# An attention and expert block on one core: gate rows computed later and stored by POOL, matmuls of ones ahead of the first data, W2 copies moved to VectorE, a re-spaced drain without activation-table changes

## The chip, the core and the metric

The kernel runs on one core of a Trainium2 chip. Five engines read their own instruction streams in order: PE (TensorE, with its weight loads shown as PEld), DVE (VectorE), ACT (ScalarE), POOL (GpSimd) and SP (SyncE, which here only issues transfers). The metric is device time in microseconds (us) of one launch, less is better. The median of 11 runs before the change is 1141.42 us (1139.15 to 1143.66).

## What is computed

32 sequences of 256 tokens with 128 channels pass an attention half and a mixture-of-experts half, both steered by six rows of a small modulation matrix. Cut to what matters:

```python
mod = (silu(c) @ wmod).reshape(32, 6, 1, 128)
sa, ca, ga, sb, cb, gb = mod[:, 0], ..., mod[:, 5]
ga = (2 * (ga >= 0) - 1) * maximum(abs(ga), 0.25)
gb = (2 * (gb >= 0) - 1) * maximum(abs(gb), 0.25)
h = layernorm(x) * (1 + ca) + sa
x = x + ga * attention(h, wq, wk, wv, wo)      # 8 heads, rms norm and rotation of q and k, causal softmax
h = layernorm(x) * (1 + cb) + sb
# experts: 8, hidden size 512, each token goes to its 2 best
scores = softmax(h @ Wr + br); weights = softmax over the two best scores
x = x + gb * sum_e weights_e * (gelu(h @ W1_e + b1_e) @ W2_e + b2_e)
```

All of it is float32 with 8192 tokens in all.

## The kernel before

The 32 sequences form 16 blocks of 512 tokens (`NBLK`). The order in which every engine gets its work is written by hand: the string `PERIOD` lists some 450 steps, each with a key (sequence of the block, group of four heads, q or k, tile of 128 tokens) and a number `-1`, `-2`, `-3` that says how many blocks it runs behind. One pass through the string is one period; the loop makes 17 of them. What stands early in the string stands early in each engine's queue, and since the queues are in order, a step that waits holds all that its engine was given after it.

The steps that matter below: `PJ` (L461, PE) projects q or k of 128 tokens and four heads; `SQ` (L467, ACT) squares it; `XX` (L475, DVE) multiplies it by cosines and sines into a tile `xx` with two buffers; `ROT` (L492, POOL) adds the halves into `rot`, which frees `xx`; `SC` (L509, POOL) scales q; `TR` (L516, PE) transposes `rot`, `ZT` (L522, ACT) copies it out; `S`, `EX`, `AV` (L536, L564, L573 to L575) are scores, exponential and the product with the values; `RES` (L600, L601, POOL) multiplies by the gate row and adds the residual.

Start. `modulate` makes the two rows that the first norm needs (L251). Right behind it `gates_of` multiplies the other four rows (L257, PE), copies them out (L259, ACT), forms the gates in six POOL instructions (L260 to L269) and stores them as `mod_rows` from ACT's queue (L270). SP loads them back per sequence (`LR`, L415), and its queue goes on in the order: two `rows` loads, then `load_rest` with Wr, br, b1 (L229), lanes, rows, then the next sequences. POOL copies b1 into the tile of the expert weights (L232) behind the first `ROT` of the second head group. `turn_values` and `merge_values` (L276 to L284) multiply wv and wo together once.

Experts. Each token's row is stored into DRAM lists by expert, by a POOL scatter (`LS`, L320, 8 per block). From the lengths of the lists two tables are made that say which tile of 256 list rows belongs to which expert: `first_table` on POOL during the last two full periods (L906 to L976 and the `table` function, L919 to L960), `second_table` on DVE later. 71 tiles follow (`tile_step`): SP loads the rows, PE transposes them, four hidden matmuls with W1 (L1081), gelu on ACT (L1082), the product with W2 (L1109), on DVE the bias and the weight (L1086 to L1097), two scatters into `results` by POOL (L320). The expert's W1 is copied to a working tile by ACT (L1047), its W2 by POOL (L1052, 128x640), one tile ahead. The first 41 tiles (`FULL`) take from the first table.

The last block's routing (logits `LG`, `lg`, `mx`, `sub`, `exp`, `sum`, `rcp`, `sc`, then the two picks `s0` to `p1`, the weights `e0`, `e1`, `w0`, `w1`, the places) is laid between the first tiles by the string `DRAIN`, a group a tile. `exp` (L681) and `e1` (L768) use ACT's exponential, whereas the tiles use gelu. The lists of the block before the last are stored there too (`delayed`).

Of the kernel before, what the change touches and what calls it, by code (L numbers as in the profile page):

```python
# [11 lines left out]
F32 = mybir.dt.float32  # L12
# [3 lines left out]
ALU = mybir.AluOpType  # L16
# [3 lines left out]
P = 128  # L20
# [41 lines left out]
| AV.112 EX.113 RD.112 ST.112 H2.0 | AV.113 RD.113 ST.113  # L62
| HT.0 PAY.0 RES.1 HC.0 | M1.1 | M2.1 MB.1 | M3.1 | H2.1 | HT.1 PAY.1 | HC.1 LS.6-1 | LG LS.7-1
| lg mx sub | exp | sum rcp sc s0 | d0 k0 m0 p0 sc2 | s1 d1 k1 m1 e0 | p1 sel e1 | PC w0 w1 pay2
| len place pp | to LS.0 | | LS.1 | | LS.2 | | LS.3 | | LS.4 | | LS.5 | LS.6 | | LS.7
"""
# [3 lines left out]
def kernel(  # L70
# [49 lines left out]
    FW = FC * P  # L120
    LOADS = 4


# [6 lines left out]
    assert DONE[0] <= FULL and (EARLY - LAST[0]) * K * TB > E * (TS - 1)  # L130
    DONE[0] = FULL + E - 1

    const = ctx.enter_context(tc.tile_pool(name="const", bufs=1))
# [28 lines left out]
    minus_half = const.tile([P, 1], F32)  # L162
    nc.vector.memset(minus_half, -0.5)


# [88 lines left out]

    def gates_of(mps):
        pg = mps.tile([B, 4, M], F32, tag="pj", name="pg")
        nc.tensor.matmul(pg, sg, wmod_sb[:, 2 * M :], start=True, stop=True)  # L257
        g = g_sb[0:B, 0:4, :]
        nc.scalar.copy(g, pg)  # L259
        nc.gpsimd.tensor_scalar_add(g[:, 2, :], g[:, 2, :], 1.0)  # L260


        gates = g[:, ::3, :]
        mag, sgn = gate_sb[0:B, 0:2, :], gate_sb[0:B, 2:4, :]
        nc.gpsimd.tensor_scalar(sgn, gates, 0.0, 2.0, ALU.is_ge, ALU.mult)
        nc.gpsimd.tensor_scalar_add(sgn, sgn, -1.0)
        nc.gpsimd.tensor_mul(mag, sgn, gates)
        nc.gpsimd.tensor_scalar_max(mag, mag, 0.25)
        nc.gpsimd.tensor_mul(gates, sgn, mag)  # L269
        nc.scalar.dma_start(mod_rows, g)  # L270

# [62 lines left out]
    with ExitStack() as pa:  # L334
# [68 lines left out]
        class Steps:  # L403
# [276 lines left out]
            def exp(blk):  # L680
                nc.scalar.activation(held["sc", blk], held["sc", blk], AF.Exp)  # L681

# [83 lines left out]
            def e1(blk):  # L766
                e = keep(sm, [P, 2, NTB], "e", blk)
                nc.scalar.activation(e[:, 0], held.pop(("e0", blk)).squeeze(2), AF.Exp)  # L768
                nc.scalar.activation(e[:, 1], e[:, 0], AF.Identity, bias=ones[:, 0:1])

            def w0(blk):
                nc.vector.reciprocal(held["pay", blk][:, :, 0, M + 1], held["e", blk][:, 1])

            def w1(blk):
                pay = held["pay", blk]
                nc.gpsimd.tensor_mul(
                    pay[:, :, 1, M + 1], held.pop(("e", blk))[:, 0], pay[:, :, 0, M + 1]
                )
# [86 lines left out]
        load_table()  # L865
        Steps.LX(0, 0)
        nc.sync.dma_start(cT_sb, cT)
        nc.sync.dma_start(wmod_sb, wmod)
# [6 lines left out]
        for step in first[3:]:  # L875
            step(0, 0)
        gates_of(ps_pj)

# [20 lines left out]
        def small(name, shape, dtype=F32):  # L899
            return tab.tile(shape, dtype, name=name)  # L900

        def tile_counts(eng, counts, blk, full):


            half, whole = 0.5 - 0.5 / TS, 1.5 * 2.0**23
            eng.tensor_scalar(  # L906
                counts, lengths[:, blk, :], 1.0 / TS, -half if full else half, ALU.mult, ALU.add
            )
            eng.tensor_scalar_add(counts, counts, whole)
            eng.tensor_scalar_add(counts, counts, -whole)  # L910

        def table(eng, name, bounds, n):
# [7 lines left out]

            pad = 1 << (S * E - 1).bit_length() - 1
            sums = [small(f"{name}_sums{i}", [P, pad + S * E]) for i in range(2)]
            for i in range(2):
                eng.memset(sums[i][:, 0 : pad + 1], 0.0)
            eng.tensor_copy(sums[0][:, pad + 1 :], counts.rearrange(flat)[:, 0 : S * E - 1])
            yield
            d = 1
            while d < S * E:
                old, new = sums
                eng.tensor_add(new[:, pad:], old[:, pad:], old[:, pad - d : pad - d + S * E])  # L930
                sums = [new, old]
                d *= 2
                if d in (4, 16):
                    yield
            ahead = held[name + "_ahead"] = sums[0][:, pad:].rearrange("p (s e) -> p s e", e=E)
            held[name + "_counts"] = counts
            yield
            nth = tab.tile(shape, F32, tag="nth", name="nth")
            eng.tensor_scalar(nth, ahead, -1.0, lane, ALU.mult, ALU.add)
            is_its = tab.tile(shape, F32, tag="is_its", name="is_its")  # L940
            eng.tensor_sub(is_its, nth, counts)
            eng.tensor_scalar(is_its, is_its, 0.0, None, ALU.is_lt)
            begun = tab.tile(shape, F32, tag="begun", name="begun")
            eng.tensor_scalar(begun, nth, 0.0, None, ALU.is_ge)
            eng.tensor_mul(is_its, is_its, begun)
            yield
# [8 lines left out]
            yield  # L955
            eng.tensor_mul(each, each, is_its.rearrange(flat).unsqueeze(1).to_broadcast([P, 3, S * E]))
            its = small(name + "_its", [P, 3])
# [4 lines left out]
            yield  # L962

        def first_table():
            eng = nc.gpsimd
            bounds = small("full", [P, 3, E])
            eng.memset(bounds[:, 0], 0.0)
            tile_counts(eng, bounds[:, 2], EARLY, True)
            yield
            tile_counts(eng, bounds[:, 1], LAST[0], False)  # L970
            yield

            less = small("less", [P, E])
            eng.tensor_sub(less, bounds[:, 1], bounds[:, 2])
            eng.tensor_scalar_max(less, less, 0.0)
            eng.tensor_sub(bounds[:, 1], bounds[:, 1], less)  # L976
            yield
            yield from table(eng, "first", bounds, lengths[:, EARLY, :])

        def second_table():  # L980
# [10 lines left out]
            for i, blk in enumerate(LAST):  # L991
                tile_counts(eng, bounds[:, i + 1], blk, False)
                if i == 0:
                    eng.tensor_tensor(bounds[:, 1], bounds[:, 1], bounds[:, 0], ALU.max)
                if i % 2 == 0:
                    yield
# [51 lines left out]

        def weights_2(i):
            e = number(i, 1, mybir.EngineType.Pool, E - 1)  # L1050
            w2s[i] = wk2.tile([P, FW + M], F32, tag="sq", name="w2")
            nc.gpsimd.tensor_copy(w2s[i], W2_sb[:, ds(e, 1), :].squeeze(1))  # L1052

# [64 lines left out]
        def tile_step(i, between=()):  # L1118
            if 0 <= i + LOADS < NTI:
                load(i + LOADS)  # L1120
            if 0 <= i + 1 < NTI:
                weights_2(i + 1)
            if 0 <= i < NTI:
                hidden(i, between)
            if 0 <= i + 1 < NTI:
                rows_in(i + 1)
            if 0 <= i + 2 < NTI and i >= 0:
                weights_1(i + 2)
            if 1 <= i:
                rows_out(i - 1)  # L1130
            if 0 <= i < NTI:
                second(i)
# [39 lines left out]
        def issue(steps):  # L1172
# [9 lines left out]
            (0, 0, 1, 1): [(turn_values, 1), (merge_values, 0)],  # L1182
            (0, 1, 0, 0): [(merge_values, 1)],
        }
        waiting, delayed = [], []
        for n in range(NBLK + 1):
            if n == 1:
                load_rest()
            if n == 3:
                load_experts()  # L1190
            for j, (step, key, behind) in enumerate(period):
                blk = n - behind
                if not 0 <= blk < NBLK or (blk == 0 and step in first and key == [0]):
                    pass
                elif blk == 0 and step in (Steps.V, Steps.VC) and waiting is not None:
                    waiting.append((step, key))
                elif n == NBLK and blk == NBLK - 2 and step is Steps.LS:
                    delayed.append((step, key, NBLK - 1 - blk))
                else:
                    step(blk, *key)  # L1200
                if blk == 0 and step is Steps.PJ:
                    for aside, g in besides.pop(tuple(key), ()):
                        aside(ps_s, g)
                    if not besides and waiting is not None:
                        for aside, k in waiting:
                            aside(0, *k)
                        waiting = None
                if NBLK - 2 <= n < NBLK and j % 48 == 47:
# [12 lines left out]
        for i in range(NTI + 1):  # L1221
# [4 lines left out]
            if held.get("lengths"):  # L1226
                next(tables, None)
                next(ends, None)
            issue(delayed[i : i + 1])
            if i + 3 < len(drain):  # L1230
# [83 lines left out]
```

## Time and profile before

| | |
|---|---|
| median of 11 runs | 1141.42 us |
| profiled execution, time | 1140.71 us |
| its span, first to last instruction | 1138.5 us |
| mean granted TensorE clock | 0.994 |
| PE busy | 1098.8 us (97%) |
| POOL busy | 963.5 us (85%) |
| DVE busy | 959.4 us (84%) |
| ACT busy | 870.9 us (76%) |

The page divides the span into 40 equal slices and gives each engine's busy share of a slice as a digit. A row of a timeline reads: start in us, duration in us, engine, line, operation, what is written and from what, the count of merged instructions, and in brackets the idle time before it with what ended it. A row of a table by stages gives, for a stretch of the span, each engine's busy us and the count of its instructions, then the granted clock, the share of the DMA engines and GB/s. A row of a list of waits gives who waited for whom, the total in us, the number of times and the longest.

### The profile page before, as it was taken

Reading aid. Unit: us, or ns where it says so; the run is one execution under the profiler, and the core shown is the slowest. Engines: PE = TensorE matmul, PEld = TensorE weight load, DVE = VectorE, ACT = ScalarE, POOL = GpSimd, SP = SyncE. Lnnn points to the kernel's source line nnn. Section 1 sums busy time; section 2 is a strip of 40 time slices with the busy share of each in tenths; the row PEclk is TensorE's granted clock in tenths of the full one; section 3 lists DMA queues with packets and bytes.
Section 4 is the critical chain, followed back from the end, with each engine's and each line's share of the span. In section 5 each row is a group of like instructions: output and inputs, shape, how many; then the busy total and the mean of one; then the engine's idle time right before and its main releaser. Section 6 shows DMA issues by size and latency. Waiting matters only on the chain.

```text
span 1138.5 us, 22160 instructions
## 1 busy us (share of the span) xinstructions
PE 1098.8 (97%) x6566; PEld 859.4 (75%) x6566; DVE 959.4 (84%) x2582; ACT 870.9 (76%) x2244; POOL 963.5 (85%) x1257
## 2 busy tenths in 40 slices
PE   6999999999999999999999999998998999999994
PEld 3777777777777777777777777676787889999994
DVE  3989999999999999999999999998973465445895
ACT  4878888888878888888878888787875776766762
POOL 5768989898989989898989989998957788877775
PEclk9999999999999999999999999999999999999998
DMA  4005101010000101000000100001002243224785
GB/s 149 1 13 177 33 23 28 18 30 22 24 25 20 31 23 29 17 29 22 24 26 19 31 22 26 17 31 37 13 6 65 66 106 92 79 73 113 230 230 147
DMA packets 70102, 61.69 MB, mean 54 GB/s; under 512 B 8627, under 2 KB 60468, under 8 KB 69984
## 3 DMA queue, kind: packets, MB, share of 16 engines
q1 hardware_dynamic: 52832, 39.09, 12.8%
q0 software_dynamic: 8640, 16.93, 4.4%
q10 hardware_dynamic: 8512, 4.26, 1.3%
q8 instruction: 53, 0.87, 0.3%
q14 instruction: 65, 0.53, 0.2%
HBM read 38.01 MB, written 23.15 MB: 54 GB/s over the span
## 4 chain that ended last, share of the span: by engine, by line
PE 79%; DVE 6%; POOL 6%; DMA 5%; issue 3%; ACT 1%; SPq 0%; POOLq 0%; DVEq 0%; ACTq 0%
PE pj L461 17%; PE s L536 13%; PE ptr L516 9%; PE pj L449 9%; PE py L1109 7%; PE ph L1081 7%; PE o L573 5%; PE o L575 5%; PE o L574 5%; DMA results<-yo,to 2%; DMA y<-results 2%; POOL rot L492 1%; POOL results L320 1%; PE pm L659 1%; POOL rot L509 1%
## 5 line engine op out<-in xcount | busy, mean ns | idle before, releaser
L492 POOL TENSOR_TENSOR rot<-xx 128x512 f32<-128x512 f32 x256 | 323.6, 1274 | 23.5 <-DVE xx L475 14.5
L475 DVE TENSOR_TENSOR xx<-pj,rope_sb 128x1024 f32<-128x1024 f32 x256 | 310.9, 1215 | 12.4 <-ACT sq L467 8.1
L461 PE MATMUL pj<-wqk_sb,hT 128*128 128x512 f32 x512 | 261.0, 597 | 4.1 <-DVE xx L475 4.1
L564 ACT ACTIVATE p<-s,rn 128x256 f32<-128x256 f32 (+1 forms) x512 | 188.1, 422 | 49.2 <-DVE s L557 43.2
L536 PEld LDWEIGHTS s<-zT,zT 128*128 128x128 f32 x1024 | 179.7, 191 | 51.4 <-issue 34.1
L536 PE MATMUL s<-zT,zT 128*128 128x256 f32 (+1 forms) x1024 | 207.6, 328 | 0.0
L467 ACT ACTIVATE sq<-pj 128x512 f32<-128x512 f32 x256 | 153.6, 600 | 55.7 <-PE pj L461 42.7
L320 POOL DMA_INDIRECT results<-yo,to x142 | 145.0, 1021 | 44.2 <-issue 18.0
L1082 ACT ACTIVATE hid<-ph,w 128x256 f32<-128x256 f32 x284 | 124.7, 473 | 75.2 <-PE ph L1081 74.0
L485 DVE TENSOR_REDUCE ss<-sq 128x4 f32<-128x512 f32 x256 | 172.2, 674 | 3.2 <-ACT sq L467 3.2
L516 PEld LDWEIGHTS ptr<-ident,rot 128*128 128x128 f32 x1024 | 120.5, 141 | 54.3 <-issue 34.7
L522 ACT COPY zT<-ptr 128x512 f32<-128x512 f32 x256 | 146.5, 589 | 11.9 <-PE ptr L516 11.9
L320 POOL DMA_INDIRECT lists<-pay,to x128 | 128.6, 1004 | 30.1 <-issue 14.2
L573 PEld LDWEIGHTS o<-vx,p 128*128 128x128 f32 x512 | 87.0, 190 | 87.3 <-issue 39.9
L516 PE MATMUL ptr<-ident,rot 128*128 128x128 f32 x1024 | 146.9, 273 | 1.8 <-POOL rot L492 1.8
L1109 PE MATMUL py<-w,hid 128*128 128x128 f32 x1136 | 138.9, 275 | 3.5 <-POOL w L1052 1.6
L592 DVE SCALAR_TENSOR_TENSOR attn<-o,rd,attn 128x128 f32<-128x128 f32 x448 | 135.7, 344 | 5.3
L1109 PEld LDWEIGHTS py<-w,hid 128*128 128x128 f32 x1136 | 132.5, 192 | 4.5 <-POOL w L1052 3.4
L1081 PE MATMUL ph<-hT,w 128*128 128x256 f32 x568 | 134.7, 380 | 0.0
L449 PE MATMUL pj<-wvo_sb,hT 128*128 128x512 f32 x256 | 132.2, 599 | 1.2 <-ACT vx L455 0.7
L509 POOL TENSOR_TENSOR rot<-rot,rn 128x512 f32<-128x512 f32 x128 | 131.1, 1041 | 1.3 <-ACT rn L504 0.7
L1081 PEld LDWEIGHTS ph<-hT,w 128*128 128x128 f32 x568 | 102.4, 190 | 10.9
(186 smaller groups left out, 1793.0 us busy)
## 6 DMA issues: line engine op xcount, KB each, us to landing
xt<-lists SPq DMA_DIRECT2D x71, 130.0 KB, 2.6
y<-results SPq DMA_DIRECT2D x15, 512.0 KB, 5.1
rows<-mod_rows SPq DMA_DIRECT2D x32, 192.0 KB, 3.1
xt<-in_x_dram SPq DMA_DIRECT2D x32, 128.0 KB, 2.1
out_dram<-ot ACTq DMA_DIRECT2D x15, 256.0 KB, 3.5
results<-yo,to POOLq DMA_INDIRECT x142, 2.5
W_sb<-in_W_dram SPq DMA_DIRECT2D x1, 2048.0 KB
W_sb<-in_W_dram SPq DMA_DIRECT2D x8, 256.0 KB, 12.0
```

Source lines behind the costliest of these rows:

```text
L320: return nc.gpsimd.indirect_dma_start(out=out, out_offset=bass.IndirectOffsetOnAxis(ap=to, axis=0), in_=src, in_offset=None, bounds_check= ...
L449: nc.tensor.matmul(pv, held["hT", b][:, ts(t, P)], wvo_sb[:, ts(g, HG * P)], start=True, stop=True)
L461: nc.tensor.matmul(pj, held["hT", b][:, ts(t, P)], wqk_sb[:, w, ts(g, HG * P)], start=True, stop=True)
L467: nc.scalar.activation(keep(wk2, [P, HG, P], "sq", b, g, w, t), held["pj", b, g, w, t], AF.Square)
L475: nc.vector.tensor_mul(keep(wk2, [P, 2, HG, P], "xx", b, g, w, t), held.pop(("pj", b, g, w, t)).unsqueeze(1).to_broadcast([P, 2, HG, P]), ...
L485: nc.vector.tensor_reduce(held["ss", b, g, w][:, t, :], held.pop(("sq", b, g, w, t)), AX.X, ALU.add)
L492: nc.gpsimd.tensor_add(keep(wk2, [P, HG, P], f"rot{w}", b, g, t, bufs=4).rearrange(halves, two=2), xx[:, 0].rearrange(halves, two=2), xx[: ...
L516: nc.tensor.transpose(ptr[:, h, :], rot[:, h, :], ident)
L536: nc.tensor.matmul(s[:, cols, :], kT[:, h, keys], qT[:, h, keys.start :], start=True, stop=True)
L564: nc.scalar.activation(p[:, cols, :], s[:, cols, :], AF.Exp, scale=rk[:, t, h : h + 1])
L1081: nc.tensor.matmul(ph, w1[:, ts(f, P)], hT, start=True, stop=True)
L1109: nc.tensor.matmul(pys[i][:, t, :], hid[:, f, ts(t, P)], w2[:, ts(f, P)], start=(f == 0 and t == 0), stop=(f == FC - 1), skip_group_check= ...
```

## The change

The changes, in the order of the program:

- The constant `euler` is set on DVE, and eight 128x128 matmuls of ones by ones are issued on PE ahead of everything, right after the first x load is issued.
- `gates_of` leaves the start. It is called after the projection with key (0, 1, 1, 1), the last of the first sequence's, takes a PSUM buffer of the tag "s", and stores `mod_rows` from POOL's queue. The two `rows` loads of block 0 are issued after it; on SP's queue they stand where they stood, ahead of `load_rest`.
- The buffers of the tables are cleared in `tables_begin`, after `load_rest`; on POOL these five memsets come right behind the copy of b1. The tables take one call of `tile_counts` for two rows, and a shorter test (3 instructions for 5) for which tile belongs to a lane.
- W2 is copied by DVE for the first 41 tiles, behind `rows_out` of the tile before the last; POOL keeps it for the others.
- `DRAIN` is re-spaced. The first three list stores of the block before the last go before the drain, the others later and the last block's sooner. `exp` of the last block becomes a power of e on POOL; its `e1` becomes a tanh on ACT. ACT's queue then has no table load behind the first gelu.

```diff
 DRAIN = """
...
-| HT.0 PAY.0 RES.1 HC.0 | M1.1 | M2.1 MB.1 | M3.1 | H2.1 | HT.1 PAY.1 | HC.1 LS.6-1 | LG LS.7-1
-| lg mx sub | exp | sum rcp sc s0 | d0 k0 m0 p0 sc2 | s1 d1 k1 m1 e0 | p1 sel e1 | PC w0 w1 pay2
-| len place pp | to LS.0 | | LS.1 | | LS.2 | | LS.3 | | LS.4 | | LS.5 | LS.6 | | LS.7
+| HT.0 PAY.0 RES.1 HC.0 | M1.1 M2.1 MB.1 | M3.1 H2.1 | HT.1 PAY.1 | HC.1 | LG | lg mx sub exp sum
+| rcp sc s0 LS.6-1 | d0 k0 m0 p0 sc2 LS.7-1 | s1 d1 k1 m1 e0 | p1 sel e1 | PC w0 w1 pay2 |
+| len place pp | to LS.0 | LS.1 | | LS.2 | LS.3 | | LS.4 | LS.5 | | LS.6 | LS.7
 """
...
-    def gates_of(mps):
-        pg = mps.tile([B, 4, M], F32, tag="pj", name="pg")
+    def gates_of(mps, _):
+        pg = mps.tile([B, 4, M], F32, tag="s", name="pg")
...
-        nc.scalar.dma_start(mod_rows, g)
+        nc.gpsimd.dma_start(mod_rows, g)
...
             def exp(blk):
-                nc.scalar.activation(held["sc", blk], held["sc", blk], AF.Exp)
+                sc = held["sc", blk]
+                if blk < NBLK - 1:
+                    nc.scalar.activation(sc, sc, AF.Exp)
+                else:
+                    nc.gpsimd.tensor_tensor(
+                        sc, euler.unsqueeze(1).to_broadcast(over_e), sc, ALU.pow
+                    )
...
             def e1(blk):
                 e = keep(sm, [P, 2, NTB], "e", blk)
+                if blk == NBLK - 1:
+                    nc.scalar.activation(e[:, 0], held.pop(("e0", blk)).squeeze(2), AF.Tanh, scale=0.5)
+                    return
...
         Steps.LX(0, 0)
+        pm = ps_pj.tile([P, HG, P], F32, tag="pj", name="warm")
+        for i in range(WARM):
+            nc.tensor.matmul(pm[:, i % HG, :], ones, ones, start=True, stop=True)
         nc.sync.dma_start(cT_sb, cT)
...
         for step in first[3:]:
             step(0, 0)
-        gates_of(ps_pj)
...
+            begun = tab.tile([P, width], F32, tag="begun", name="begun")
+            eng.tensor_scalar(begun, befores, lane, None, ALU.is_le)
+            is_its = tab.tile([P, S * E], F32, tag="is_its", name="is_its")
+            eng.tensor_sub(is_its, begun[:, 0 : S * E], begun[:, 1:])
             nth = tab.tile(shape, F32, tag="nth", name="nth")
             eng.tensor_scalar(nth, ahead, -1.0, lane, ALU.mult, ALU.add)
-            is_its = tab.tile(shape, F32, tag="is_its", name="is_its")
-            eng.tensor_sub(is_its, nth, counts)
-            eng.tensor_scalar(is_its, is_its, 0.0, None, ALU.is_lt)
-            begun = tab.tile(shape, F32, tag="begun", name="begun")
-            eng.tensor_scalar(begun, nth, 0.0, None, ALU.is_ge)
-            eng.tensor_mul(is_its, is_its, begun)
...
+        def tables_begin():
+            for name, S in (("first", 2), ("second", len(LAST))):
+                pad = 1 << (S * E - 1).bit_length() - 1
+                held[name + "_sums"] = [
+                    small(f"{name}_sums{i}", [P, pad + S * E + 1]) for i in range(2)
+                ]
+                for tile in held[name + "_sums"]:
+                    nc.gpsimd.memset(tile[:, 0 : pad + 1], 0.0)
+            held["full"] = small("full", [P, 3, E])
+            nc.gpsimd.memset(held["full"][:, 0], 0.0)
...
-        def weights_2(i):
-            e = number(i, 1, mybir.EngineType.Pool, E - 1)
+        def weights_2(i, engine):
+            e = number(i, 1, engine.engine, E - 1)
             w2s[i] = wk2.tile([P, FW + M], F32, tag="sq", name="w2")
-            nc.gpsimd.tensor_copy(w2s[i], W2_sb[:, ds(e, 1), :].squeeze(1))
+            engine.tensor_copy(w2s[i], W2_sb[:, ds(e, 1), :].squeeze(1))
...
-            if 0 <= i + 1 < NTI:
-                weights_2(i + 1)
+            if FULL <= i + 1 < NTI:
+                weights_2(i + 1, nc.gpsimd)
...
             if 1 <= i:
                 rows_out(i - 1)
+
+            if 0 <= i + 1 < FULL:
+                weights_2(i + 1, nc.vector)
...
+            (0, 1, 1, 1): [(gates_of, None)],
         }
+        besides_of = {Steps.V: (0, 1, 0, 0), Steps.VC: (0, 1, 0, 0), Steps.LR: (0, 1, 1, 1)}
...
             if n == 1:
                 load_rest()
+                tables_begin()
...
-                elif n == NBLK and blk == NBLK - 2 and step is Steps.LS:
+                elif n == NBLK and blk == NBLK - 2 and step is Steps.LS and key[0] > 2:
                     delayed.append((step, key, NBLK - 1 - blk))
...
-            issue(delayed[i : i + 1])
+            if i > 2:
+                issue(delayed[i - 3 : i - 2])
```

## The prediction

> **What bounds the kernel now.** First the stages: busy us by engine (PE, PEld, DVE, ACT, POOL), granted clock, DMA share, GB/s.
>
> ```profile
> 36.00:700.00 664.00, 664.00 (x3798) 491.67 (x3796) 639.13 (x1617) 548.19 (x1460) 597.22 (x784) 1.00 0.10 30
> 700.00:810.00 110.00, 104.84 (x587) 75.02 (x586) 100.04 (x254) 84.79 (x226) 99.94 (x152) 1.00 0.10 28
> 845.00:918.00 73.00, 66.12 (x459) 60.48 (x460) 31.56 (x126) 52.11 (x117) 54.76 (x73) 1.00 0.23 61
> 918.00:1047.00 129.00, 129.00 (x897) 120.02 (x896) 69.06 (x272) 89.19 (x208) 102.14 (x116) 1.00 0.32 87
> ```
>
> PE has no gap from 36 to 700 us: what delays it before 36 comes out at the end us for us. It loses 5.2 us while POOL makes the first table, 6.9 us while the drain runs between the first tiles, nothing in the tiles after. Then the start, in the timeline.
>
> ```profile
> 9.62 0.56 POOL L260 TENSOR_SCALAR x<-x 32x128 f32<-32x128 f32 x1 [4.47 <-ACT x L259]
> ...
> 13.59 0.18 DVE L371 BATCH_NORM_AGGREGATE xn_mv<-xn_st 128x2 f32<-128x6 f32 x1
> 14.00 0.71 POOL L269 TENSOR_TENSOR x<-x 32x256 f32<-32x256 f32 x1
> 14.74 0.35 ACTq L270 DMA_DIRECT2D mod_rows<-x  x1
> 15.15 0.30 ACT L375 ACTIVATE xn_rs<-xn_mv,eps_ln 128x2 f32<-128x2 f32 x1 [5.62 <-POOL x L269]
> ...
> 16.41 0.81 SPq L415 DMA_DIRECT2D rows<-mod_rows  x2
> ...
> 18.21 0.43 SPq L229 DMA_DIRECT2D b_sb<-in_b1T_dram  x1
> ...
> 30.57 0.22 POOL L232 COPY W_sb<-b_sb 128x32 f32<-128x32 f32 x1
> ...
> 30.99 1.02 PE L461 MATMUL pj<-wqk_sb,hT 128*128 128x512 f32 x2
> ...
> 31.67 2.50 POOL L492 TENSOR_TENSOR rot<-xx 128x512 f32<-128x512 f32 x2 [0.88 <-DVE xx L475]
> ...
> 35.75 0.60 PE L516 MATMUL ptr<-ident,rot 128*128 128x128 f32 x4
> ```
>
> ACT's store (L270) waits for the gates and holds ACT's queue; SP's `rows` wait for the store. PE's row at 35.75 transposes the second of the two `rot` made at 31.67. Two rows of the clock, and the PE waits of the drain:
>
> ```profile
> 18.00:19.00 1.00, 1.00 (x4) 0.52 (x3) 1.00 (x2) 0.00 (x0) 0.77 (x1) 0.62 0.76 237
> ...
> 20.00:21.00 1.00, 1.00 (x7) 1.00 (x7) 0.00 (x0) 0.31 (x1) 0.49 (x1) 0.50 0.62 131
> ```
>
> ```profile
> PE pm L648 <- POOL pay L634: 3.2, 1, 3.2
> PE py L1109 <- POOL w L1052: 1.6, 2, 1.5
> PE py L1109 <- DVE py L1086: 1.1, 1, 1.1
> PE py L1109 <- issue: 0.8, 1, 0.8
> ```
>
> **The change, part by part.** I write times of the old execution; a minus is a gain.
>
> *A, the store leaves ACT.* ACT's L375 started at 15.15 for the store's sake; its input was ready at 13.77 (13.59 + 0.18), because that x lands only at 12.87. So 1.35 us are gained, not the whole 5.6 us wait. Against it stands the clock: PE idled from 13.38 to 17.47 and got 0.50 from about 18.4 to 21.8. Now its early work is done sooner, by about 11.2 (wv lands at 3.73 + 7.0 = 10.7), and it idles 4.9 us to 16.1. If half speed then covers the 2.3 us to 18.4 too, some 1.15 us of work are lost. A lies between -1.35 and -0.2; I take -0.7, the middle. The eight matmuls of ones run where PE has nothing (its first work is at 5.53) and cost nothing.
>
> The Trainium skill ("TensorE: Matmul & The Clock Gate", practical table at its end) warns of PE gaps above some 3 us between bursts, which return the clock to half; the 4.1 us gap here agrees. By it the warmth bought before 5.5 us is lost again ahead of 16 us, and A would be near its upper end.
>
> *B, the gates in POOL's queue.* This decides. The new `pg` stands behind PE's L461 of 30.99: 31.85 to 32.9. ACT copies it by 33.45 (0.57 as at L259). POOL's six instructions took 9.62 to 14.71, so 33.55 to 38.64, and the store starts at 38.7. POOL waits from 28.4 with its next `ROT` behind. The store lands 2.5 us later (POOL's scatters into `results`, median; ACT's store took 16.38 - 14.74 = 1.64): 41.2. Now a ring closes: SP's queue has `rows` first, which wait for the store, and b1 behind; b1 was issued 1.83 us after the landing (18.21 - 16.38) and takes 2.9 us to land, so 45.9. POOL's copy L232 waits for b1, and behind it stand five memsets (0.1 each) and the two `ROT`s that PE needs. Copy 0.2, memsets 0.4, two `ROT`s 2.5: 49.0. PE's transposes of 35.75 start there: +13.3 us. The bounds are a store of 1.64 and of 2.7 us: 12.4 and 13.5. DVE cannot hide it, `XX` needs the `xx` buffer that the held `ROT` frees. PE's other delays (0.86 for `pg`, 2 us for `hT` behind ACT's copy) end under this wait. Other loads behind `rows` (the x of block 1, needed at 44.74 + 13) come in time.
>
> *C, the clock after that gap.* PE stands 11 us, far more than the 4.1 us that cost the clock before. The old rows of 0.62, 0.50, 0.50 and 0.68 sum to a loss of 0.38 + 0.5 + 0.5 + 0.32 = 1.7 us. Bounds: 0, if POOL and DVE (0.9 and 0.65 us further behind PE than before at the restart) would hold it anyway, and twice 1.7. I take +1.7.
>
> *D, the first table.* Gone on POOL: one group of three counts (710.79 to 711.63, 0.84), three small rows (0.18 with the gap), two tests (0.6) and two memsets (0.14), 1.75 us. POOL is 91% busy there, and PE's recurring row of four L461 records, otherwise 51.17 us apart, came at 648.25, 754.00 and 809.68, so 7.9 us late against about 8.3 us of table work: nearly one to one. -1.7, bounds 0 and -2.8 (POOL's 1.1 us wait for `first_its` gone as well).
>
> *E, the drain.* Removed at best: the four waits shown, 6.7 us. New: the longer chain per tile. `sum`, `s0`, `k0`, `k1` follow in four neighbouring tiles, and in each DVE waits until POOL has put out two scatters (2.3 us) and one small operation, after 1.75 us of its own `yo` work: 4.9 to 5.4 us a tile against PE's 3.735. DVE may lag 3.9 us before PE's `py` has no buffer. The first step starts with POOL some 1.9 us behind; the four lags leave 3.2 us of PE waiting. The earlier `HT.1` waits for `pay` about 0.6, the copies ahead of the last `AV` about 0.7. The power:
>
> ```profile
> 864.53 0.73 POOL L617 TENSOR_TENSOR x1n_rs<-x1n_rs,minus_half 128x2 f32<-128x2 f32 x1
> ...
> 919.66 0.99 DVE L987 TENSOR_SCALAR done<-done 128x16 f32<-128x16 f32 x1
> ```
>
> It has 2 columns at 0.73, where a plain operation has 0.24; the new one has 32: 0.75 if all is fixed, 0.24 + 32 x 0.245 = 8.1 if all is per column. Nearest is the row of the same operation, so I take 1.5, which adds 0.75. E = -6.7 + 3.2 + 1.3 + 0.75 = -1.5, bounds -6.7 and +5.
>
> *F, W2 on DVE.* A copy is bounded by 0.28 (128x128 from SBUF, L1000) and 640/1024 of an `XX`, 0.76, plus a wait for POOL such as the 0.99 of L987, whose like take 0.17. With `yo`'s 1.8 us a tile that is at most 3.4 under PE's 3.735: 0, hidden by PE's matmuls. Uncovered it would be where the second table fills DVE (918 to 929): up to +3.
>
> "SBUF — State Buffer" of the skill (the box on SWDGE, and "Who interferes with whom") says that a DVE copy between SBUF tiles keeps POOL from writing descriptors until it ends, with 3.1 us for a 0.62 us transfer. No row here shows a scatter so stretched. By it each of 41 tiles would have POOL later; two scatters fill 2.6 of 3.7 us, so a stretch above 1.1 us a tile would reach PE.
>
> Sum: -0.7 + 13.3 + 1.7 - 1.7 - 1.5 = +11.1. The profiled execution took 1140.7 (span 1138.5), 0.7 under the median: 1151.8, against the median about 1152.
>
> **Rivals.**
> *R1, the steady periods take the delay back* (the faster side). If PE's 664 busy us hide slack (the ends are modelled, PEld is 74% busy), thirteen periods could win back B and C; from 1.2 us a period on, nothing is left and A, D, E give 1141.4 - 3.9 = 1137.5. Against it: the same PE row recurs every 51.16 or 51.17 us, and DVE stands at 96%. Chance 0.06.
> *R2, b1 isn't waited for.* Then POOL goes on at 39.7 and is done at 39.7 + 1.3 + 0.6 + 2.5 = 44.1: B is 8.4, the time 1147. For: in the old run L232 never waited. Against: SP is in order and b1 stands behind `rows`. Chance 0.12.
> *R3, power or contention hold the drain*: E at +5, 1158; above that with F. Chance 0.12.
> *R4, the warm clock survives to 16 us and the restart costs nothing*: A -1.35, C 0, time 1149.5; within the forecast's range.
>
> **How the numbers follow.** The forecast, the ring through b1, has 0.70: 1147 to 1156. Range 1144 to 1158, which takes in R2 and a drain that gains all. 0.2% (2.3 us) is about what a measurement can tell from no change. Faster 0.06 (R1), within 0.2% 0.05 (R2 with the full gain of the drain), slower 0.89.
>
> **What would show it.** PE's longest wait, near 38 to 49 us, put down to POOL's `rot`; POOL's copy of b1 waiting for a transfer until about 45, with the `rows` loads ahead of it; a clock of 0.50 behind it; periods of 51.17 again; no table load after the first gelu. A PE gap below 6 us there makes me wrong, as does a drain whose PE loss falls to 1 us with a cheap power, or periods that shorten.

## The result, and the profile after

The changed kernel takes 1148.72 us (median of 8 runs, 1146.82 to 1149.82) where the kernel before takes 1140.82 (31 runs): a ratio of 1.0065, 95% interval 1.0056 to 1.0074. It is slower by 7.9 us. Its profiled execution has a span of 1146.2 us (before 1138.5) and a mean granted clock of 0.986 (before 0.994).

The first view is the table by stages of the changed kernel; as before, each row gives the stretch, the busy us of PE, PEld, DVE, ACT and POOL, then the granted clock, the DMA share and GB/s.

```profile
36.00:60.00 24.00, 15.10 (x60) 10.17 (x61) 13.04 (x24) 7.50 (x16) 15.02 (x21) 0.79 0.19 52
60.00:710.00 650.00, 650.00 (x3724) 481.99 (x3723) 626.14 (x1590) 538.68 (x1439) 585.70 (x771) 1.00 0.10 30
710.00:820.00 110.00, 108.29 (x611) 78.51 (x610) 102.55 (x263) 87.38 (x235) 102.47 (x152) 1.00 0.10 29
...
855.00:925.00 70.00, 65.13 (x440) 59.69 (x441) 41.91 (x147) 45.76 (x108) 47.85 (x55) 0.98 0.21 59
925.00:1055.00 130.00, 130.00 (x909) 121.21 (x908) 78.09 (x284) 89.18 (x209) 83.25 (x89) 1.00 0.31 84
```

PE now loses 8.9 us between 36 and 60, where before it lost nothing after 36. From 60 to 710 it is full in both. While the first table is made it loses 1.7 us (before 5.2), in the drain 4.9 (before 6.9), in the tiles after it nothing. The start, in the timeline of the changed kernel:

```profile
38.31 0.78 POOL L274 DMA_DIRECT2D mod_rows<-x  x1 [0.32 <-POOL x L273]
...
40.43 1.22 DVE L479 TENSOR_TENSOR xx<-pj,rope_sb 128x1024 f32<-128x1024 f32 x1 [9.62 <-POOL rot L496]
40.46 0.82 SPq L419 DMA_DIRECT2D rows<-mod_rows  x2
...
41.80 2.05 PE L465 MATMUL pj<-wqk_sb,hT 128*128 128x512 f32 x2 [7.71 <-DVE xx L479]
...
42.26 0.43 SPq L233 DMA_DIRECT2D b_sb<-in_b1T_dram  x1
...
46.04 0.21 POOL L236 COPY W_sb<-b_sb 128x32 f32<-128x32 f32 x1 [5.64 <-DMA b_sb<-in_b1T_dram]
...
46.45 2.47 POOL L496 TENSOR_TENSOR rot<-xx 128x512 f32<-128x512 f32 x2
...
48.98 1.11 PE L520 MATMUL ptr<-ident,rot 128*128 128x128 f32 x4 [3.10 <-POOL rot L496]
```

Read it from the bottom. PE's transposes, which came at 35.75, wait for POOL's two `rot`; these stand behind the copy of b1, which waits 5.64 us for a transfer that SP issued only after `rows`, and `rows` waited for POOL's store. PE has a second, longer wait in the same gap: 7.71 us for DVE's `xx`, which had no buffer (DVE's row at 40.43) until POOL was done with the gates. POOL stood 5.27 us for ACT's copy of `pg`, with the `ROT`s behind it in its queue, and then made the gates from 32.91 to 37.99. Third, the drain: first the waits of PE in it, then the rows around the longest one.

```profile
PE py L1146 <- DVE mx L697: 2.9, 1, 2.9
...
PE py L1146 <- DVE s L707: 0.8, 1, 0.8
...
PE py L1146 <- DVE pick L731: 0.3, 1, 0.3
```

```profile
887.45 5.46 POOL L689 TENSOR_TENSOR sc<-euler,sc 128x32 f32<-128x32 f32 x1
...
892.94 0.18 DVE L694 TENSOR_REDUCE mx<-sc 128x4 f32<-128x32 f32 x1 [8.26 <-POOL sc L689]
...
895.41 3.51 PE L1146 MATMUL py<-w,hid 128*128 128x128 f32 x16 [2.89 <-DVE mx L697]
```

The power takes 5.46 us on POOL. DVE stands idle 8.26 us for it and for the two scatters that POOL had ahead of it, with `yo` of a finished tile and the next W2 copy behind it in its queue, so PE has no W2 (the profile puts PE's wait down to L697, which stands right behind that copy). The four waits of the drain that the prediction shows are gone from the list. When PE goes on, its 16 matmuls take 3.51 us where the others take 1.95: half clock.

To place the rest, four rows that recur in every trace are compared: PE's two transposes of block 1's first `xn`, the first and the last first-matmul of a tile, and the span (all in us).

| kernel | `xn` of block 1 | first tile | last tile | last - first | span |
|---|---|---|---|---|---|
| before | 57.31 | 847.58 | 1119.68 | 272.10 | 1138.5 |
| changed | 72.07 | 857.86 | 1128.82 | 270.96 | 1146.2 |
| difference | +14.76 | +10.28 | +9.14 | -1.14 | +7.7 |

So the start costs 14.8 us, and 4.5 come back before the first tile: 0.3 in the steady periods (the row of eight L540 at 683.54 against 669.05, +14.49) and 4.2 while the first table is made (840.79 against 830.47, +10.32). The drain and the tiles give 1.1, and what lies behind the last tile's matmuls 1.4.

### The profile page after: what moved, and what is told of

The parts are those of the page before. It is cut to its first block, busy times and chain, and to the rows that moved or that the text cites. A ratio compares the mean times of both kernels' runs of the same rounds, so it can differ in the third digit from the quotient of the medians.

```text
span 1146.2 us, 22146 instructions
## 1 busy us (share of the span) xinstructions
PE 1106.0 (96%) x6582; PEld 865.8 (76%) x6582; DVE 975.5 (85%) x2620; ACT 865.2 (75%) x2238; POOL 941.7 (82%) x1215
## 4 chain that ended last, share of the span: by engine, by line
PE 85%; DVE 5%; POOL 5%; DMA 2%; issue 1%; ACT 1%; SPq 0%; DVEq 0%; POOLq 0%; ACTq 0%
PE pj L465 17%; PE s L540 13%; PE py L1146 10%; PE ph L1118 9%; PE ptr L520 9%; PE pj L453 9%; PE o L577 5%; PE o L579 5%; PE o L578 5%; POOL rot L496 1%; PE pt L1104 1%; DVE xx L479 1%; PE pm L663 1%; DMA xt<-in_x_dram 1%; DVE attn L596 1%
## 5 line engine op out<-in xcount | busy, mean ns | idle before, releaser
L496 POOL TENSOR_TENSOR rot<-xx 128x512 f32<-128x512 f32 x256 | 323.6, 1274 | 23.3 <-DVE xx L479 14.8
L465 PE MATMUL pj<-wqk_sb,hT 128*128 128x512 f32 x512 | 264.5, 605 | 12.3 <-DVE xx L479 11.4
L540 PEld LDWEIGHTS s<-zT,zT 128*128 128x128 f32 x1024 | 180.5, 191 | 52.1 <-issue 34.5
L540 PE MATMUL s<-zT,zT 128*128 128x256 f32 (+1 forms) x1024 | 208.4, 329 | 0.0
L324 POOL DMA_INDIRECT results<-yo,to x142 | 148.0, 1042 | 70.5 <-DVE yo L1134 44.2
L526 ACT COPY zT<-ptr 128x512 f32<-128x512 f32 x256 | 146.6, 589 | 11.1 <-PE ptr L520 11.1
L513 POOL TENSOR_TENSOR rot<-rot,rn 128x512 f32<-128x512 f32 x128 | 131.2, 1042 | 1.1 <-ACT rn L508 0.7
```

Of the source, the lines that this page charges most:

```text
L324: return nc.gpsimd.indirect_dma_start(out=out, out_offset=bass.IndirectOffsetOnAxis(ap=to, axis=0), in_=src, in_offset=None, bounds_check= ...
L465: nc.tensor.matmul(pj, held["hT", b][:, ts(t, P)], wqk_sb[:, w, ts(g, HG * P)], start=True, stop=True)
L496: nc.gpsimd.tensor_add(keep(wk2, [P, HG, P], f"rot{w}", b, g, t, bufs=4).rearrange(halves, two=2), xx[:, 0].rearrange(halves, two=2), xx[: ...
L540: nc.tensor.matmul(s[:, cols, :], kT[:, h, keys], qT[:, h, keys.start :], start=True, stop=True)
```

## The experiments

In the first two groups of runs (e1 to e4, and the control with e5 to e7) the kernel before took 1155.5 and 1155.1 us, in the last two 1140.9 and 1142.2. The traces of the first two groups show ScalarE standing up to 4.5 us (e3) at several places of the drain and the tiles behind it, put down to no instruction of the program; the difference from the first to the last tile's first matmul is 283 to 290 us in all of them. The second and third groups ran on the same chip, so the chip alone doesn't explain the stalls; their cause stays open. Times are therefore compared within a group, and across groups by their ratios or by rows ahead of the first tile. The control's trace, ACT around one such place:

```profile
881.36 0.47 ACT L1119 ACTIVATE hid<-ph,w 128x256 f32<-128x256 f32 x1 [0.95 <-remote]
883.51 0.47 ACT L1119 ACTIVATE hid<-ph,w 128x256 f32<-128x256 f32 x1 [1.68 <-remote]
```

All edits below are against the changed kernel.

**The control**, the changed kernel itself in the second group.

> The changed kernel itself, as the control for the three runs beside it, since chips differ: 1.0065 times the kernel before. If the early PE wait before 16 us comes out under 3.5 us and the clock then stays at 1.00 until the gap at 33 us, some 2 us less (as it did in e2 and e4 and not in e1 and e3).

1165.37 us, ratio 1.0100 (1.0073 to 1.0128), 10.3 us over the kernel before where the result has 7.9. Its early PE wait is 3.30 us, the clock stays at 1.00 behind it, and `xn` comes at 70.90. The ratio missed the 1.0065; of the 2 us expected from the kept clock 1.2 are there (72.07 - 70.90).

**e1: the gates first again.**

```diff
...
         for step in first[3:]:
             step(0, 0)
+        gates_of(ps_pj)
...
-            (0, 1, 1, 1): [(gates_of, None)],
...
-        besides_of = {Steps.V: (0, 1, 0, 0), Steps.VC: (0, 1, 0, 0), Steps.LR: (0, 1, 1, 1)}
+        besides_of = {Steps.V: (0, 1, 0, 0), Steps.VC: (0, 1, 0, 0)}
```

> The changed kernel with the gates back at the start, still stored by POOL; all else as changed. My theory: the whole start loss (14.8 us by the recurring PE rows, with A's gain of 0.75 in it) is the gates' place, so 1148.7 - 14.8 - 0.75 = 1133.2 us (1132.2 to 1134.5), faster than both kernels, and no PE wait above 3 us between 30 and 60 us. Rival: the early PE work and the clock it loses cause a good part of the start loss; then 1138 or more.

1152.1 us, ratio 0.9975 (0.9962 to 0.9988): the time in us missed in a group with stalls. The control is of another group: by the ratios e1 is 0.0125 under it, some 14.4 us, and by `xn` 14.3. `xn` comes at 56.58, 0.73 ahead of the kernel before, and PE has no wait at all between 30 and 60 us. The gates' place is the whole of the start's loss, and the store in POOL's queue alone costs nothing: it is A's gain that is left.

**e2: the copy of b1 later.** The DMA stays where it is.

```diff
         nc.sync.dma_start(rows_sb, rows)
+    def copy_b1():
         nc.gpsimd.tensor_copy(W_sb[:, :, FW : FW + FC], b1_sb)
...
             if n == 3:
+                copy_b1()
                 load_experts()
```

> The changed kernel with POOL's copy of b1 issued with the expert weights, two blocks later; the gates stay late. The ring theory: POOL's two ROTs end about 43.3 instead of 48.9, PE still has its scores until 45.9, so PE's 3.1 us wait for rot goes, and with it about 1.3 us of half clock behind it: 1144.3 us (1143.5 to 1145.8); the 7.7 us wait of PE for xx stays. Rival (R2 as told in the prediction: b1 isn't what POOL's second pair of ROTs waits for): 1148.7.

1162.88 us, ratio 1.0072 (1.0057 to 1.0088). The row of `xn` stands at 66.08, 4.8 before the control and e4 (70.86, of e2's own group), which both had the same clock ahead of the gap. The trace of e2, POOL and PE:

```profile
38.44 2.50 POOL L498 TENSOR_TENSOR rot<-xx 128x512 f32<-128x512 f32 x2
```

```profile
39.66 2.05 PE L467 MATMUL pj<-wqk_sb,hT 128*128 128x512 f32 x2 [7.71 <-DVE xx L481]
41.50 2.77 PE L542 MATMUL s<-zT,zT 128*128 128x256 f32 x8
44.06 1.06 PE L522 MATMUL ptr<-ident,rot 128*128 128x128 f32 x4
```

The `rot` come 2.3 us behind the store (36.17) instead of 8.1, and the transposes follow the scores without a wait. The ring through b1 is real, and worth 4.8 us by the row of `xn`. By the ratios it is 0.0028, some 3.2 us, but their intervals overlap, so the size rests on the rows of three traces. That b1 isn't waited for (R2) is out. The 7.71 us for `xx` stay.

**e3: the exponential by ScalarE again.**

```diff
-                if blk < NBLK - 1:
-                    nc.scalar.activation(sc, sc, AF.Exp)
-                else:
-                    nc.gpsimd.tensor_tensor(
-                        sc, euler.unsqueeze(1).to_broadcast(over_e), sc, ALU.pow
-                    )
+                nc.scalar.activation(sc, sc, AF.Exp)
```

> The changed kernel with the last block's exponential by ScalarE again (its tanh stays). Theory: the power is the drain's loss, 2.9 us of PE wait and 1.5 us of a slower py behind it; an ACT exponential costs two table loads of 1.28 us, of which 0 to 2 us reach PE: 1148.7 - 4.4 + 1 = 1145.3 us (1144.3 to 1146.5). Rival, the prediction's own sizes (power 0.75, the four lags 3.2): 1148 or more, and the PE wait for DVE stays above 2 us.

1166.9 us (1157.15 to 1169.0), ratio 1.0088 (1.0058 to 1.0119): inconclusive. The stalls stood just ahead of the router, and `xn` came at 73.69 because the early clock was lost here and kept in the control.

**e4: no matmuls of ones.**

```diff
-        pm = ps_pj.tile([P, HG, P], F32, tag="pj", name="warm")
-        for i in range(WARM):
-            nc.tensor.matmul(pm[:, i % HG, :], ones, ones, start=True, stop=True)
```

> The changed kernel without the eight matmuls of ones. Theory: the clock falls to 0.50 at 8 us and at 15 us all the same, so nothing is lost: 1148.7 us, within 0.6. Rival (R4, the warm clock is kept and spares something): up to 1.2 us slower, 1149.9.

1166.55 us (1164.94 to 1170.29), ratio 1.0112 (1.0094 to 1.0131), beside the control's 1.0100 with an overlapping interval. `xn` comes at 70.86 against the control's 70.90. The ones do nothing, and e4 without them kept the full clock from 15 to 21 us that the changed kernel's first profile had lost with them. R4 is out in what it says of the ones: the clock was kept in e4 without them as in the control and e2 with them. It is out in the restart too, which still cost time there (*C* below).

**e5 and e9: the exponential from tanh**, tried in the second group and again in the third.

```diff
-                    nc.gpsimd.tensor_tensor(
-                        sc, euler.unsqueeze(1).to_broadcast(over_e), sc, ALU.pow
-                    )
+                    up = sm.tile(over_e, F32, tag="up", name="up", bufs=1)
+                    nc.scalar.activation(sc, sc, AF.Tanh, scale=0.5)
+                    nc.vector.tensor_scalar(up, sc, -1.0, 1.0, ALU.mult, ALU.add)
+                    nc.vector.reciprocal(up, up)
+                    nc.vector.scalar_tensor_tensor(sc, sc, 1.0, up, ALU.add, ALU.mult)
```

> The changed kernel with the last block's exponential made from ScalarE's tanh, e^x = (1+t)/(1-t) with t = tanh(x/2): one ACT and three small DVE operations (0.2 each) in place of POOL's power of 5.46 us, and no table load. Theory: the power costs 2.9 us of PE wait and 1.5 us of half clock, so 4.4 us less than the control (3 to 5). Rival (the four lags of the chain hold PE, not the power): within 1 us of the control.

1166.69 us, ratio 1.0102 (1.0080 to 1.0123): nearer the rival, 1.3 us over the control. In the control's trace PE doesn't wait for `mx` although DVE waits 7.24 us for the power. A stall just ahead of the router had put PE back by some 3.3 us, and the eight matmuls that follow took 3.76 us for 1.89, which would give DVE the time; with that reading e5 was run again:

> e5 again. In the changed kernel's first profile PE waited 2.9 us on the power and ran 1.5 us slower behind it; in the control's and in e5's profiles ScalarE stalls of 1 to 1.7 us just ahead of the router left PE a tile at half clock, 1.9 us slower, which covers the power. Theory: without these stalls the ratio is 1.0065 - 4.4/1141 = 1.0026 (1.0015 to 1.004); with them it is that of e5, 1.010. Rival (the power costs nothing either way): 1.0065 without stalls.

1144.65 us, ratio 1.0034 (1.0023 to 1.0044): 4.1 us under the changed kernel's 1148.72, 3.5 by the ratios. From the first to the last tile it takes 266.54 us for 270.96: 4.4 less. The PE waits of e9 from 855 to 930:

```profile
PE o L577 <- DVE attn L596: 0.8, 2, 0.4
PE py L1148 <- DVE s L709: 0.6, 1, 0.6
PE py L1148 <- ACT hT L1108: 0.6, 1, 0.6
```

The wait for `mx` is gone; of the chain's lags 0.6 us for `s` is left, and 0.6 for ACT's `hT`. The power costs 3.5 to 4.4 us.

**e6 and e10: gates first and tanh**, the two edits of e1 and e5 together.

> The changed kernel with the gates at the start (stored by POOL) and the exponential from tanh. If the two losses are independent: 15.3 + 4.4 us under the control, which is 11.8 us under the kernel before, ratio 0.990 (0.988 to 0.992). Rival (what the power's place hides comes back as another wait of the drain): only the gates' share, 0.994.

1149.49 us, ratio 0.9954 (0.9936 to 0.9972), 15.9 under the control: short of both ratios that were expected. That is little more than the 15.3 expected of the gates, of the power's 4.4 hardly anything can be seen, and the trace has the stalls again.

> e6 again: gates at the start, exponential from tanh, W2 by DVE as in the change. From e8's start (first tile at 842.3 us) and e9's tiles (266.5 us from the first tile's first matmul to the last tile's, where e8 with W2 by POOL took 270.9): 842.4 + 266.5 + 17.5 us behind it + 2.1 us outside the span = 1128.5 us, ratio 0.989 (0.988 to 0.9905) where ScalarE has no stalls of its own. Rival (W2 by DVE spares nothing): that of e8, 0.993.

1128.99 us, ratio 0.9881 (0.9864 to 0.9897): 13.2 us under the kernel before, and the best of all. Its first tile stands at 843.08, its last at 1109.68 (266.60). The two losses are independent, as the sum had it.

**e7 and e11: all copies of W2 by POOL**, and **e8**, the same with the edits of e6.

```diff
-            if FULL <= i + 1 < NTI:
+            if 0 <= i + 1 < NTI:
                 weights_2(i + 1, nc.gpsimd)
...
-            if 0 <= i + 1 < FULL:
-                weights_2(i + 1, nc.vector)
```

> The changed kernel with all copies of W2 by POOL again. Theory: DVE's copies are hidden by PE's matmuls, and on POOL they lie beside scatters that fill 2.6 of 3.7 us: within 1 us of the control, at most 2 us slower while lists and results are scattered together. Rival (a DVE copy holds up POOL's scatters, so that DVE's copies cost more than they spare): faster than the control by 1 us or more.

1162.83 us, ratio 1.0067 (1.0048 to 1.0085), 2.5 under the control, as the rival had it.

> Gates at the start, exponential from tanh, and all copies of W2 by POOL: is the copy by DVE a loss of its own? If the 2.5 us that e7 was under its control are the copies' (a DVE copy that holds scatters, or DVE's lag), 2.5 us under e6, ratio 0.993. If e7's gain came from the start's clock or the stalls of ScalarE, the same as e6: 0.9954 within 0.0015.

1132.96 us, ratio 0.9932 (0.9919 to 0.9946). The number is the first theory's, but its comparison, e6, was of the group with stalls; beside e10's 0.9881 it is a loss of 0.0051, some 5.8 us (the medians differ by 4.0), and from the first to the last tile e8 takes 270.87 us where e9 and e10 take 266.54 and 266.60. So the disagreement was run once more:

> e7 again: the changed kernel with W2 by POOL alone. By e8 against e9, POOL's copies hold the router's small operations and then ScalarE's queue: 1148.7 + 2 to 4 us where ScalarE has no stalls of its own, ratio 1.0065 + 0.0025 = 1.009 (1.008 to 1.0105). Rival (e7's 2.5 us gain is the copies'): 1.0043.

1153.69 us, ratio 1.0103 (1.0086 to 1.0119), 0.38% or 4.3 us above the changed kernel's ratio. From the first to the last tile: 275.43 against 270.96. In e11 DVE's longest wait from 855 to 930, and PE's longest behind the start:

```profile
DVE mx L694 <- POOL sc L689: 11.8, 1, 11.8
```

```profile
PE py L1146 <- DVE mx L697: 5.4, 1, 5.4
```

DVE waits 11.8 us against the changed kernel's 8.26, PE 5.4 against 2.9: the copies stand ahead of the router's small operations in POOL's queue. In e8, without the power, the lag reaches PE through ScalarE, whose `hid` it awaits for 2.4 us. Copies of W2 by DVE spare 4.3 to 4.5 us with the power (e11), and without it (e10 against e8) 4.3 by the tiles, 4.0 by the medians and 5.8 by the ratios. Why e7 gained in the group with stalls stays open.

## Why the prediction was right, and which terms were not

The forecast was 1152 us in 1144 to 1158; the time is 1148.72, 3.3 under it, and as a difference +7.9 where +11.1 was forecast. Its main step is the one that happened; some terms were mis-sized, and that two of them cancel is luck. The miss is mostly *D* (2.5 us) and what lies behind the last tile (1.4).

| term | forecast | measured | from |
|---|---|---|---|
| A, B, C: the start | +14.3 | +14.8 | `xn` of block 1 |
| steady periods | 0 | -0.3 | row of eight L540 |
| D, first table | -1.7 | -4.2 | the same row, three periods on |
| E and F, drain and W2 | -1.5 | -1.1 | last - first tile |
| behind the last tile | 0 | -1.4 | to the end of the span |
| sum | +11.1 | +7.7 | span |

*A* was right in this profile: the first transposes of `rot`, which come ahead of the gates, stand 0.78 before the old ones (26.74 against 27.52); e1 gives 0.73. ACT's L379 started 1.51 us sooner (13.64 against 15.15), and the half clock took the rest. But the size hangs on the clock. In the three traces that kept it (control, e2, e4) the same transposes stand 2.9 to 3.2 us ahead, beyond the bound of -1.35, which had taken the old kernel's own stretch of half clock as a loss that stays. (That stretch is 18.23 to 21.65 in the record of the clock; I had read 18.4 to 21.8.) The ones cost and bring nothing (e4).

*B, the ring,* came step by step: store at 38.31 (38.7), landed at 40.44 (41.2), b1's copy at 46.04 (45.9), transposes at 48.98 (49.0). So close a fit is partly luck: the store landed in 2.1 us where I took 2.5, b1 in 3.7 where I took 2.9. As A's 0.78 is in the measured rows, B itself is 14.0. What I put wrongly is the share: PE had another wait of 7.7 us in the same gap, for `xx`. I had named its cause, the held `rot`, only as a reason why DVE can't hide the gap. So of the gap the ring is some 4.8 us (e2), and the rest is POOL's wait for `pg` and the gates' work in its queue, which no longer lies where POOL was idle. R2 had priced just that, 8.4 without the ring, which leaves 4.9 for the ring. That the ring alone decides was too simple; that the sum is the gates' place is shown (e1).

*C* was right: from the transposes to `xn` the changed kernel takes 23.09 us (72.07 - 48.98) and the kernel before 21.56 (57.31 - 35.75), 1.5 more. It too hangs on the clock: the same stretch takes 24.08 in the control, where half clock lasts until 51.88, and 21.62 in e11, where it has ended at 46.77, ahead of the transposes (47.91).

*D* failed at its lower bound. "Gone on POOL" counted 1.75 us and let only the 1.1 us wait for `first_its` go besides. That wait fell to 0.30, and a wait of POOL's `sel` for DVE (1.38 at 782.19 before) isn't there at 794.24 after. 1.75 + 0.8 + 1.38 = 3.9 us, near the 4.2; that `sel`'s wait went because of the sooner table is argued, not tried, and no run brings the old table back. PE's own rows agree: in this stage its waits for POOL's `rot`, `p` and `sel` were 1.8, 0.6 and 0.6 us before, and 0.3 for `rot` alone after. (The three rows of L461 that the prediction names stand 0.16 us sooner in the timeline, 648.09, 753.84 and 809.52; their distances are as given.) Thirteen profiles with the new table take 195.3 to 195.6 us from the row of four L465 near 650 to the first tile, the kernel before 199.5.

*E* failed in the price of the power. "I take 1.5" because the nearest row was the same operation; it took 5.46, within the bounds of 0.75 and 8.1, and cost 3.5 to 4.4 us of the path (e9); the profile has 2.9 as a wait and 1.6 as half clock behind it. The row at 128x2 had 0.73, so by these two rows an estimate is (5.46 - 0.73)/30 = 0.16 us a column and some 0.4 fixed: the size belonged between the bounds, nearer the upper one. The four lags, priced at 3.2, came to 1.1 (0.8 + 0.3). Without the power and with W2 on POOL (e8) the tiles take 270.87 us, 1.2 less than before, where my terms without the power come to -2.2.

*F* failed in its sign. "0, hidden by PE's matmuls" looked at DVE's load alone. The gain is on POOL, where the copies stood ahead of the router's operations: some -4.3 us (e11, and e8 against e10). The copy itself takes 0.535 us on DVE and 0.73 on POOL. E without F is thus some +3.2 and F -4.3, where I had -1.5 and 0: two errors of 4 to 5 us that hide each other in the table's row of -1.1. The rule of the Trainium skill that I weighed ("SBUF — State Buffer", "Who interferes with whom"), by which a DVE copy keeps POOL from its descriptors, does not show: a scatter into `results` takes 1042 ns on average in the changed kernel, and 1053 in e11 and 1021 in the kernel before, both without DVE copies. In the changed kernel the 36 scatters that overlap a DVE copy in time have a median of 972 ns, the other 106 one of 976.

R1 is out: the periods are 51.13 to 51.16 us, before 51.16 to 51.18, and twelve of them win back 0.3. R3 came in part, as the power, without reaching +5. The 1.4 us behind the last tile was in no term: 17.4 us to the end of the span against 18.8, and 17.3 to 18.5 in the twelve traces of the other runs; with a single trace of the kernel before it stays open whether the change did that.

## What to carry to other kernels

Work moved off the start must be followed through every in-order queue that it enters: here a store on POOL, two loads on SP and a copy on POOL closed a ring, and even with the ring cut the gates held POOL where PE waited for it. When a price is known only from a tiny shape, the size has to be taken between the bounds by columns, not by the name of the operation. An engine's copy is judged by what stands behind it in its queue, not by its own load: W2 on DVE is worth 4 us because POOL's small operations come sooner. And the start of such a kernel is read from several traces, not one: with the clock, the same code's start moved by 4.2 us here, about as much as any of the later terms.

## What the runs showed of the hardware

The clock behind the early PE gap didn't follow the length of the wait. Waits of 3.12 (e4), 3.30 (control) and 3.50 us (e2) kept 1.00, while 2.25 (e5), 2.26 (e7), 3.40 (e8), 3.67 (changed), 3.96 us (e1) and all longer ones were followed by 0.50. A row of the changed kernel's profile, and the same of e4's:

```profile
17.00:19.00 2.00, 2.00 (x8) 1.38 (x7) 1.23 (x2) 0.06 (x1) 1.54 (x2) 0.50 0.00 0
```

```profile
17.00:19.00 2.00, 2.00 (x15) 1.52 (x14) 0.99 (x2) 1.37 (x3) 1.30 (x2) 1.00 0.00 0
```

The third number from the end is the granted clock: PE is busy all the time from 17 to 19 in both, at half and at full speed, and the four transposes of L280 behind the wait take 1.06 us in the one and 0.60 in the other. In the traces' record of the clock the stretches away from the ends last 3.413 us or whole multiples of it (3.413, 6.827, 10.24, 17.07). The Trainium skill ("TensorE: Matmul & The Clock Gate", "What's actually happening") has the clock decided over a window of 3413 ns that runs freely of the kernel. These lengths agree with it.

Laid over PE's rows as a grid of steps of 3.413 us, the record shows what counted: how much of the wait fell into one step. In e2 a step ends at 14.26 us and cuts the 3.50 us into 1.74 and 1.76; the clock stayed. In e5 the whole 2.25 us lie in the step from 13.54 to 16.96, and the clock fell at its end. In the changed kernel 2.18 of the 3.67 us lie in the step that ends at 14.48, and the clock fell there, while PE still waited. Over all fourteen traces, steps at full clock with at most 1.84 us of this wait (e4) kept it, and steps with 2.18 us or more lost it. This is read off the traces and not tried by a run, and it isn't the whole rule: two steps ahead of 9 us with only 1.65 (changed) and 1.32 us (e9) of idle time, between small matmuls, were also followed by 0.50. The start of one and the same code moved by 4.2 us between seven traces (`xn` from 69.53 in e11 to 73.69 in e3).

The power on POOL at some 0.16 us a column (an estimate from two rows), the tanh in gelu's table (behind the first gelu, no trace with it shows a table load but e3's two, at its exponential and at the gelu after it), and ScalarE's stalls in two of the four groups, which hid the power's cost, were not expected either.
